# Graph attention at the two ends of a four-layer GNN: seven of sixteen row tiles computed row by row

## The chip, the cores and the metric

One core of a Trainium2 chip runs the whole program. The metric is device time in microseconds (us) from the first instruction to the last, the median of several executions. The engines named below are TensorE (PE), VectorE (DVE), ScalarE (ACT), GpSimd (POOL), and SyncE (SP), whose queue issues nearly all DMAs.

## What is computed

Eight graphs of 2048 nodes with 128 features share one 0/1 adjacency matrix. Four layers follow each other, each as `x = x + layer(relu(layernorm(x)))`. Layers 0 and 3 are graph attention with one head, layer 1 is masked attention with four heads, and layer 2 is a mean over neighbours. Layer 3, cut to what matters (layer 0 has the same score, and adds a second normalisation, a residual and an elu):

```python
h = einsum('bni,oi->bno', x, W)
s, d = h @ a_src, h @ a_dst
e = s[:, :, None] + d[:, None, :]
e = where(e > 0, e, 0.2 * e)
e = where(adj[None] == 0, -1e9, e)
out = einsum('bij,bjf->bif', softmax(e, axis=-1), h)
```

For each of the eight graphs that is a 2048 x 2048 score matrix, made from two vectors alone. A row tile is 128 rows of it, so there are 16 row tiles.

## The kernel before

**Order of the work.** Layer 1 of graph b is the backbone ("mains"). In its gaps the kernel lays layers 2 and 3 of graph b-1 and layer 0 of graph b+1. Two stretches have no such partner: layer 0 of graph 0 at the start, and layers 2 and 3 of graph 7 at the end. They are called the two ends here. The order of instructions on PE, DVE, ACT and POOL is the order in which the Python code emits them; each engine runs its list strictly in that order. The SP queue alone is ordered by the framework. It too waits at its first instruction that isn't ready.

**Graph attention, transposed (`gat_loop`).** Row tiles are taken in six groups of 3, 3, 3, 3, 2 and 2 (`GROUPS`). The score is held with the neighbour index j on the partitions and the group's rows along the free axis, so it can be used as a matmul operand without a transpose. One step handles two column tiles j (an item; there are 8 per group) and is skewed over seven stages:

- `leaky`: two ACT instructions (Prelu of row vector `ab` plus a bias per partition), 128x384 each for a group of three.
- `lowered`: DVE subtracts the row maximum, 128x768.
- `exps`: one ACT Exp, 128x768.
- `masked`: DVE applies the FP8 mask `mg`, 128x768.
- `product`: 6 PE matmuls into `gacc`; a column of ones in `haug` gives the softmax's sum.
- `ended` and `closed`: DVE divides and adds to x (`finish`), with an ACT Exp for layer 0's elu.

Five items can be in flight (pool `gp`, tile `ge`). Ahead of each group, `ahead` computes the row maxima (`gat_maximum`, line 447: one DVE instruction over 128x2048 for each row tile, from the row vector `s2b` and the int8 mask `pmg`, which a DMA fetches into two buffers of 256 KB), then `shifts` and `spread` send two short rows through DRAM and back as `ab` (line 410), on which the group's first `leaky` waits.

**Multi-head attention, by rows.** Layer 1 holds a score with its rows on the partitions: PE makes it, one masked minimum on DVE makes mask and maximum (line 963), one ACT Exp with the sum as a by-product (line 970), then PE transposes (line 982), ACT copies the transposed tiles out of PSUM as `eT` (line 987), and PE multiplies by the values.

**The start.** DMA brings 16 adjacency tiles of 1 MB. Each is turned into an int8 mask for rows (`pm_all`) and an FP8 mask for groups (`mg_all`) by DVE, PE and ACT (lines 1181 to 1211). The last of these steps are laid among the first steps of layer 0's loop. When a quarter of x (four row tiles) has ended, `before_attention` normalises and projects it for layer 1, in six short steps: statistics (DVE), root (POOL), apply (DVE), transpose, and two projections (PE, then ACT copies). Layer 1 can begin when all four quarters are projected.

**The end.** After layer 2 of graph 7, `layer3` projects, builds `s2b`, and the loop runs to the last output DMA.

Of the kernel before, what the change touches and what calls it, by code (L numbers as in the profile page):

```python
# [9 lines left out]
F32 = mybir.dt.float32  # L10
BF16 = mybir.dt.bfloat16
FP8 = mybir.dt.float8e4
I8 = mybir.dt.int8
# [18 lines left out]
def gnn_kernel(  # L32
# [104 lines left out]
    def chunk(s):  # L137

        return new(cp, "c", s, (P, 512))
# [90 lines left out]
    for c in range(2):  # L230
        nc.vector.tensor_scalar(
            ga[:, 2 * c : 2 * c + 2], a12_0, cols[:, 2 * T + 4 + c : 2 * T + 5 + c], None, ALU.mult
        )
    ones = const.tile([P, P], F32, name="ones")
    nc.gpsimd.memset(ones, 1.0)
    pga = psum("pga", (P, 4))
    nc.tensor.matmul(pga, ones, ga, start=True, stop=True)
    gab = const.tile([P, 4], F32, name="gab")
    nc.vector.tensor_copy(gab, pga)
    w0T = const.tile([P, P], F32, name="w0T")  # L240
    pw0 = psum("pw0", (P, P))
    nc.tensor.transpose(pw0, w0[:, 0:P], ident)
    nc.vector.tensor_copy(w0T, pw0)
# [33 lines left out]
    def at(place, f):  # L277

        f.place = place
        return f  # L280
# [19 lines left out]
    def run(steps):  # L300
        for _, fns in steps:
            settle()
            for f in fns:
                f()
        settle()
# [142 lines left out]
            dump, st["s2b"], pm, UP, HIGHEST, ALU.add, ALU.min, st["mn"][:, it : it + 1]  # L448
        )

    def gat_loop(st, finish, maxima, gap):


        steps = Steps()
# [34 lines left out]
            gr[k]["s1"], gr[k]["m"] = t[:, 0 : n * P], t[:, n * P : 2 * n * P]  # L489

        def ahead(k):
            if k >= len(GROUPS):
                return []
            return [
                [lambda: fetch(k), maximum_at(k, 0)],
                [lambda: fetch_mask(k, 0), maximum_at(k, 1)],
                [maximum_at(k, 2)],
                [lambda: shifts(k)],
                [lambda: spread(k)],
            ]  # L500
# [55 lines left out]
                for f in gr.pop(k)["close"]:  # L556
                    f()

        for fns in ahead(0):
            steps.add(2.0, *fns)  # L560

        items = []
        for k in range(len(GROUPS)):
            items += [(k, jp) for jp in range(T // 2)] + [None] * gap
        stages = [leaky, lowered, exps, masked, product, ended, closed]
        names = ["leaky", "lowered", "exps", "masked", "product", "ended", "closed"]
# [1 line left out]
        for step in range(len(items) + len(stages) - 1):  # L568
            fns = []
            if step < len(items) and items[step]:  # L570
                k, jp = items[step]
                if jp == 0:
                    nxt = ahead(k + 1)
                if 0 < jp <= len(nxt):
                    fns += nxt[jp - 1]
            for s in reversed(range(len(stages))):
                if 0 <= step - s < len(items) and items[step - s]:
                    fns.append(at(names[s], lambda f=stages[s], a=items[step - s]: f(*a)))
            steps.add(2.6, *fns)
        return steps  # L580

# [70 lines left out]
            steps.add(1.0, lambda it=it: gat_maximum(st, it))  # L652
        return steps

    def layer0_loop(b, st, maxima=False, gap=1):

        xb = xs[b]

        def finish(i0, n, acc, rec):
            hq = new(hpp, "hp", "hp", (P, 3, P))  # L660
            ex = new(hpp, "ex", "ex", (P, 3, P))
# [7 lines left out]
            def add():  # L669
                for q in range(n):  # L670
                    xg = xb[(i0 + q) // 4][:, (i0 + q) % 4, :]
                    nc.vector.scalar_tensor_tensor(xg, ex[:, q, :], 1.0, xg, ALU.min, ALU.add)
                    nc.vector.scalar_tensor_tensor(xg, hq[:, q, :], 0.0, xg, ALU.max, ALU.add)

            return [add]

        return gat_loop(st, finish, maxima, gap)

    attn, ready = {}, {}

# [168 lines left out]
        agg.add(1.0, lambda: combine(G - 1))  # L849
        return steps, agg  # L850

    def layer3(b, gap=1, maxima=True):
# [24 lines left out]

        pre = Steps()
        pre.skewed(
            G,  # L880
            norm_stages(lambda g: xb[g], hdst)
            + [turned, project],
            1.0,
        )
        pre.add(0.5, settle)
        pre.add(1.0, lambda: gat_ends(st), lambda: gat_rows(st))

        def finish(i0, n, acc, rec):
            for q in range(n):
                it = i0 + q  # L890
                xg = xb[it // 4][:, it % 4, :]
                nc.vector.scalar_tensor_tensor(
                    xg, acc[:, q, 0:P], rec[:, q : q + 1], xg, ALU.mult, ALU.add
                )
                if it % 4 == 3:
                    g = it // 4
# [6 lines left out]
        tops = [at("maxi", lambda it=it: gat_maximum(st, it)) for it in range(T)]  # L903
        return pre, gat_loop(st, finish, maxima, gap), tops

# [355 lines left out]
    with tc.manual_schedule(engines=ENGINES):  # L1261
# [13 lines left out]
        rest.add(1.0, late_constants)  # L1275
        run(rest)
        xb0 = xs[0]
        loop = layer0_loop(0, st0, True)
        quarters, queue, others = before_attention(0), [], masks_all[n:]
        start = len(loop) - 9 * len(GROUPS) - 6  # L1280
        for _ in range(3):
            run([others.pop(0)])
        n_late = len(others)
        for k, step in enumerate(loop):
            run([step])
            if others and (k + 1) * n_late >= 0.1 * len(loop) * (n_late - len(others)):
                run([others.pop(0)])
            for g, group in enumerate((1, 2, 3, 5)):
                if k == start + 9 * group + 13:
                    queue.extend(quarters([g]))  # L1290
            if queue:
                run([queue.pop(0)])
        run(others + queue)

        mains = []
# [74 lines left out]
        for b in range(B):  # L1370
            side = Steps()
            if b >= 1:
                pre2, agg = layer2(b - 1)
                side.extend(pre2)
                pre3, loop3, _ = layer3(b - 1, 0)
# [41 lines left out]
            work(side, (b + 1) * per + LAG if b + 1 < B else len(mains))  # L1417
        assert not pending
        pre2, agg = layer2(B - 1)
        pre3, loop3, _ = layer3(B - 1)  # L1420

        rest = Steps(pre2)
        ahead = list(pre3)
# [57 lines left out]
```

## Time and profile before

| | |
|---|---|
| median of 3 runs | 4548.66 us (4547.9 to 4550.93) |
| the profiled execution | 4556.48 us, its span 4554.6 us |
| mean granted TensorE clock | 0.956 of full speed |
| busy over the span | PE 88%, DVE 83%, ACT 79%, POOL 12% |
| start: first `leaky` to last `masked` | 109.4 to 239.5 us |
| last row tile of layer 0 done, first Exp of layer 1 | 243.3 us, 260.75 us |
| end: `s2b` in place, first `leaky` | 4423.8 us, 4438.6 us |
| end: last `masked`, output DMA issued, span ends | 4549.1, 4551.3, 4554.6 us |

The shares over the span are an average over unlike stages; in the middle PE is busy over 90% of most slices. The two ends, 5% of the span together, have to be read by themselves, with the busy time of each engine in slices of 20 us. A group in the list of instructions shows engine, line, operation, the tile written and read, the shape, how often, the busy sum and the mean of one, and the idle time just before it with what ended that. Instructions that follow each other on an engine overlap in the records by some 0.1 us, so that the distance from start to start is a little shorter than the mean.

### The profile page before, as it was taken

How to read it: one execution, taken by the hardware profiler on the slowest of the kernel's cores; microseconds unless marked ns; L12 is line 12 of the kernel's file. 1: busy time of each engine (PE TensorE's matmuls, PEld its weight loads, DVE VectorE, ACT ScalarE, POOL GpSimd, SP SyncE). 2: the span in 40 equal slices, each digit the busy share in tenths (PEclk: the TensorE clock that was granted, in tenths of full speed). 3: DMA queues.
4: the chain of work that ended last, by engine and by line, in shares of the span. 5: the costliest groups of instructions: out<-in, count | busy, mean ns of one | idle time of the engine just before them, and what ended most of it. 6: DMA issues, size and time to landing. Idle time of an engine off the chain costs nothing.

```text
span 4554.6 us, 87375 instructions
## 1 busy us (share of the span) xinstructions
PE 4009.2 (88%) x33290; PEld 2809.7 (62%) x33290; DVE 3796.6 (83%) x7529; ACT 3613.6 (79%) x5121; POOL 553.7 (12%) x549
## 2 busy tenths in 40 slices
PE   3679998998999989998899988999899989998966
PEld 2545765666657666576666756566665766655636
DVE  5968877889889898888988889799888898748939
ACT  6658985898859888698868988598895989858916
POOL 1220011004100130002300031001300010000000
PEclk6889999999999999999999999999999999999978
DMA  8522133223241323313242232412333223222232
GB/s 305 153 69 59 54 92 110 66 71 106 82 140 53 94 83 107 109 60 105 77 128 75 67 101 84 144 49 72 102 103 116 59 69 113 58 75 71 64 100 75
DMA packets 312192, 423.32 MB, mean 93 GB/s; under 512 B 65318, under 2 KB 181724, under 8 KB 307676
## 3 DMA queue, kind: packets, MB, share of 16 engines
q1 hardware_dynamic: 311264, 417.51, 30.2%
q8 instruction: 263, 4.31, 0.4%
q14 instruction: 157, 1.29, 0.1%
q10 hardware_dynamic: 508, 0.22, 0.0%
HBM read 365.78 MB, written 55.98 MB: 93 GB/s over the span
## 4 chain that ended last, share of the span: by engine, by line
PE 31%; DVE 25%; ACT 22%; issue 5%; DMA 2%; SPq 0%; DVEq 0%; POOL 0%; ACTq 0%
PE pagg L798 7%; DVE e L963 7%; ACT e L970 6%; PE pt L982 6%; ACT eT L987 6%; PE gacc L536 6%; DVE dump L447 5%; PE sc L946 5%; ACT ge L510 5%; DVE ge L516 4%; DVE ge L525 3%; PE acc L997 3%; ACT ge L520 3%; DVE ln_s L341 1%; PE ph L397 1%
## 5 line engine op out<-in xcount | busy, mean ns | idle before, releaser
L987 ACT COPY eT<-pt 128x1024 f32<-128x1024 f32 x1024 | 996.2, 1017 | 440.8 <-PE pt L982 439.5
L536 PE MATMUL gacc<-haug,ge 128*128 128x129 f32 x8192 | 1106.6, 285 | 156.4 <-DVE ge L525 121.5
L982 PE MATMUL pt<-ident,e 128*128 128x128 f32 x8192 | 1043.7, 279 | 168.6 <-DVE amh L963 126.1
L536 PEld LDWEIGHTS gacc<-haug,ge 128*128 128x128 f32 x8192 | 1008.2, 197 | 297.7 <-issue 215.3
L982 PEld LDWEIGHTS pt<-ident,e 128*128 128x128 f32 x8192 | 928.2, 144 | 268.5 <-DVE amh L963 149.8
L970 ACT ACTIVATE e<-e,amn 128x2048 f32<-128x2048 f32 x512 | 1035.1, 2022 | 12.7 <-DVE amn L963 12.7
L510 ACT ACTIVATE ge<-ab,s 128x384 f32<-128x384 f32 (+1 forms) x1536 | 808.0, 583 | 107.7 <-DMA ab<-rowd 89.2
L963 DVE CUSTOM_DVE_ANT_0 e<-sc,pm 128x1024 f32<-128x1024 f32 x512 | 625.0, 1221 | 265.6 <-PE sc L946 220.6
L946 PE MATMUL sc<-ks,qr 32*128 32x512 f32 x4096 | 746.6, 658 | 59.5 <-ACT eT L987 41.5
L963 DVE CUSTOM_DVE_ANT_0 e<-sc,pm,amh 128x1024 f32<-128x1024 f32 x512 | 657.5, 1284 | 76.0 <-PE sc L946 3.6
L520 ACT ACTIVATE ge<-ge 128x768 f32<-128x768 f32 (+1 forms) x768 | 601.3, 784 | 134.0 <-DVE ge L516 133.1
L525 DVE SCALAR_TENSOR_TENSOR ge<-mg,ge 128x768 f32<-128x768 fp8e4 (+1 forms) x768 | 666.3, 868 | 24.4 <-ACT ge L520 23.9
L516 DVE TENSOR_TENSOR ge<-ge,ab 128x768 f32<-128x768 f32 (+1 forms) x768 | 665.7, 867 | 16.3 <-ACT ge L510 13.1
L447 DVE CUSTOM_DVE_ANT_0 dump<-s2b,pmg 128x2048 bf16<-128x2048 f32 x256 | 588.9, 2300 | 36.9 <-DMA pmg<-pm_all 18.3
L997 PE MATMUL acc<-eT,vv 128*32 128x256 f32 x8192 | 562.9, 393 | 1.9 <-ACT eT L987 1.9
L997 PEld LDWEIGHTS acc<-eT,vv 128*32 128x32 f32 x8192 | 216.3, 110 | 496.4 <-issue 407.7
L349 POOL TENSOR_SCALAR ln_r<-ln_mv 128x4 f32<-128x4 f32 x128 | 86.4, 675 | 3528.2 <-DVE ln_mv L343 3280.7
L946 PEld LDWEIGHTS sc<-ks,qr 32*128 32x128 f32 x4096 | 235.3, 187 | 222.4 <-ACT eT L987 112.6
L798 PE MATMUL pagg<-mt,hm 128*128 128x512 fp8e4 x1536 | 353.6, 380 | 11.7 <-DVE agT L816 11.7
L798 PEld LDWEIGHTS <-hm 128*128 128x128 bf16 x1536 | 148.0, 98 | 185.5 <-issue 31.4
L350 POOL TENSOR_TENSOR ln_r<-ln_r,neg_half 128x4 f32<-128x4 f32 x128 | 161.4, 1261 | 10.7
L383 PE MATMUL ptr<-ident,h 128*128 128x128 f32 x512 | 88.2, 297 | 41.1 <-DVE h L357 12.6
(131 smaller groups left out, 2591.3 us busy)
## 6 DMA issues: line engine op xcount, KB each, us to landing
pmg<-pm_all SPq DMA_DIRECT2D x256, 256.0 KB
mg<-mg_all SPq DMA_DIRECT2D x128, 384.0 KB
pm<-pm_all SPq DMA_DIRECT2D x128, 256.0 KB
qr<-qd SPq DMA_DIRECT2D x1024, 32.0 KB
mt<-mt_all SPq DMA_DIRECT2D x64, 512.0 KB
ab<-rowd SPq DMA_DIRECT2D x64, 384.0 KB
adj<-in_adj_dram SPq DMA_DIRECT2D x16, 1024.0 KB
s2b<-rowd SPq DMA_DIRECT2D x16, 1024.0 KB
```

The source lines that it names most:

```text
L447: nc.vector.tensor_tensor_reduce(dump, st["s2b"], pm, UP, HIGHEST, ALU.add, ALU.min, st["mn"][:, it : it + 1])
L510: nc.scalar.activation(e[:, c, :], gr[k]["s1"], AF.Prelu, bias=st["s2"][:, j : j + 1], alpha=ALPHA)
L516: nc.vector.tensor_tensor(e, e, bc_mid(gr[k]["m"], 2), ALU.subtract)
L525: nc.vector.scalar_tensor_tensor(e, mt, BIG, e, ALU.mult, ALU.min)
L536: nc.tensor.matmul(gr[k]["acc"][:, q, :], e[:, c, q * P : (q + 1) * P], st["haug"][:, j, :], start=(j == 0 and q == 0), stop=(j == T - 1), ...
L798: nc.tensor.matmul(st["pa"], st["hm"][:, j, s, :], st["mt", g, j // 8][:, j % 8, :], start=(j == 0 and s == 0), stop=(j == T - 1 and s == ...
L946: nc.tensor.matmul(blk["sc"][g // 2][:, (g % 2) * 512 : (g % 2 + 1) * 512], blk["q"][r, t * P : (t + 1) * P], ks_t[b, hh][r, :], start=Tru ...
L963: nc.vector.tensor_tensor_reduce(e[:, c], blk["sc"][h], pm[:, c], UP, least, ALU.add, ALU.min, to)
L970: nc.scalar.activation(blk["e"][t], blk["e"][t], AF.Exp, scale=-1.0, bias=blk["mn"][:, t : t + 1], accum_out=blk["ao"]["sum"][:, t, blk["h ...
L982: nc.tensor.transpose(pt[:, c, t, :], blk["e"][t][:, j * P : (j + 1) * P], ident)
L987: nc.scalar.copy(eT, blk.pop(("pt", w)).rearrange("p c t n -> p c (t n)"))
L997: nc.tensor.matmul(pair["acc"][g * HD : (g + 1) * HD, blk["hh"] % 2, :], vv_t[blk["b"], blk["hh"]][:, j, :], blk["eT"][w][:, g, :], start= ...
```

## The change

At both ends the loop takes groups 0, 1 and 2 only (row tiles 0 to 8). Row tiles 9 to 15 go through a new function, `gat_rowwise`. `merged` lays its steps among those of `gat_loop`, spread over 90% of it at the start and 85% at the end. The empty slot between groups (`gap`) goes from 1 to 0 there. The six middle occurrences of each loop, and all else in the middle, keep their code and their order on PE, DVE, ACT and POOL.

For a row tile, `gat_rowwise` runs one Prelu over 128x2048 from `s2b` (ACT), one masked minimum over 128x2048 in place (DVE, the same instruction form as `gat_maximum`), one Exp over 128x2048 with the sum (ACT), 16 PE transposes, two PSUM copies of 128x1024 (ACT), 16 PE matmuls into `racc`, and a `finish` for one tile.

```diff
-    ones = const.tile([P, P], F32, name="ones")
+    ones = chunk("ones")[:, 0:P]
...
-    w0T = const.tile([P, P], F32, name="w0T")
+    w0T = chunk("w0T")[:, 0:P]
...
-    def gat_loop(st, finish, maxima, gap):
+    def gat_loop(st, finish, maxima, gap, ks=range(6)):
...
+    def gat_rowwise(st, finish, its):
+        e, eT, mn, acc, close, sm_ = {}, {}, {}, {}, {}, {}
+        def leaky(it):
+            if "s1n" not in st:
+                st["s1n"] = small("s1n", (P, T))
+                nc.vector.tensor_scalar(st["s1n"], st["s1"], -ALPHA / UP, None, ALU.mult)
+            e[it] = new(ep, "e", "er", (P, N))
+            nc.scalar.activation(
+                e[it], st["s2b"], AF.Prelu, scale=ALPHA, bias=st["s1n"][:, it : it + 1],
+                alpha=1.0 / ALPHA,
+            )
+        def lowest(it):
+            pm = new(mg, "pm", "pmg", (P, N), I8)
+            nc.sync.dma_start(out=pm, in_=pm_all[it])
+            mn[it] = small("rmn", (P, 1))
+            nc.vector.tensor_tensor_reduce(
+                e[it], e[it], pm, UP, HIGHEST, ALU.add, ALU.min, mn[it]
+            )
+        def exps(it):
+            sm_[it] = small("rsum", (P, 1))
+            nc.scalar.activation(
+                e[it], e[it], AF.Exp, scale=-1.0, bias=mn.pop(it), accum_out=sm_[it]
+            )
+        def turned(it, h):
+            pt = psum("ptg", (P, 8, P))
+            for c in range(8):
+                j = 8 * h + c
+                nc.tensor.transpose(pt[:, c, :], e[it][:, j * P : (j + 1) * P], ident)
+            def read():
+                eT[it, h] = new(tp, "eT", "eTg", (P, 8, P))
+                nc.scalar.copy(eT[it, h], pt)
+            later(read)
+        def product(it, h):
+            if h == 0:
+                acc[it] = new(psa, "acc", "racc", (P, 1, P))
+            t = eT.pop((it, h))
+            for c in range(8):
+                j = 8 * h + c
+                nc.tensor.matmul(
+                    acc[it][:, 0, :], t[:, c, :], st["haug"][:, j, 0:P],
+                    start=(j == 0), stop=(j == T - 1),
+                )
+        def ended(it):
+            rec = small("rrec", (P, 1))
+            nc.vector.reciprocal(rec, sm_.pop(it))
+            close[it] = finish(it, 1, acc.pop(it), rec)
...
+        stages = [
+            (7, closed), (6, ended), (0, leaky), (1, lowest), (2, exps),
+            (3, lambda i: turned(i, 0)), (4, lambda i: turned(i, 1)),
+            (4, lambda i: product(i, 0)), (5, lambda i: product(i, 1)),
+        ]
+        for step in range(2 * len(its) + 6):
...
-        return gat_loop(st, finish, maxima, gap)
+        return merged(
+            gat_loop(st, finish, maxima, gap, ks), gat_rowwise(st, finish, rest_of(ks)), share
+        )
...
-        loop = layer0_loop(0, st0, True)
+        loop = layer0_loop(0, st0, True, 0, [0, 1, 2], 0.9)
...
-            for g, group in enumerate((1, 2, 3, 5)):
-                if k == start + 9 * group + 13:
+            for g in range(G):
+                if g not in begun and st0["ended"].issuperset(range(4 * g, 4 * g + 4)):
+                    begun.add(g)
                     queue.extend(quarters([g]))
...
-        pre3, loop3, _ = layer3(B - 1)
+        pre3, loop3 = layer3(B - 1, 0, True, [0, 1, 2], 0.85)
```

A step number in `stages` counts steps of `gat_rowwise`; a new tile starts every second step. So an even step emits, for ACT, the Prelu of tile n and the Exp of tile n-1, and an odd step emits the masked minimum of tile n. A quarter of x now starts for layer 1 as soon as its four tiles have ended; quarters 1 and 2 need group 2 and so come last, one behind the other. Layer 3's output DMAs follow the same test.

More of the change, by code (lines that the diff above doesn't have):

```diff
@@ L491, in ahead @@
         def ahead(k):
-            if k >= len(GROUPS):
-                return []
             return [
@@ L557, in closed @@
                     f()
-        for fns in ahead(0):
+        for fns in ahead(ks[0]):
             steps.add(2.0, *fns)
         items = []
-        for k in range(len(GROUPS)):
+        for k in ks:
             items += [(k, jp) for jp in range(T // 2)] + [None] * gap
@@ L572, in gat_loop @@
                 if jp == 0:
-                    nxt = ahead(k + 1)
+                    nxt = ahead(ks[ks.index(k) + 1]) if k != ks[-1] else []
                 if 0 < jp <= len(nxt):
@@ L578, in gat_loop, with rest_of, closed @@
                     fns.append(at(names[s], lambda f=stages[s], a=items[step - s]: f(*a)))
+            steps.add(2.6, *fns)
+        return steps
+    def rest_of(ks):
+        its = set(range(T))
+        for k in ks:
+            its -= set(range(GROUPS[k][0], sum(GROUPS[k])))
+        return sorted(its)
+    def gat_rowwise(st, finish, its):
[44 more added lines that the diff above has]
+            close[it] = finish(it, 1, acc.pop(it), rec)
+        def closed(it):
+            for f in close.pop(it):
+                f()
+        stages = [
[3 more added lines that the diff above has]
+        ]
+        steps = Steps()
+        for step in range(2 * len(its) + 6):
+            fns = [
+                lambda f=f, i=its[(step - s) // 2]: f(i)
+                for s, f in stages
+                if (step - s) % 2 == 0 and 0 <= (step - s) // 2 < len(its)
+            ]
@@ L653, in layer0_maxima, with layer0_loop @@
         return steps
-    def layer0_loop(b, st, maxima=False, gap=1):
+    def layer0_loop(b, st, maxima=False, gap=1, ks=None, share=1.0):
         xb = xs[b]
         def finish(i0, n, acc, rec):
-            hq = new(hpp, "hp", "hp", (P, 3, P))
-            ex = new(hpp, "ex", "ex", (P, 3, P))
+            if n > 1:
+                hq = new(hpp, "hp", "hp", (P, 3, P))
+                ex = new(hpp, "ex", "ex", (P, 3, P))
+            else:
+                t = chunk("hp1")
+                hq, ex = (t[:, c * P : (c + 1) * P].unsqueeze(1) for c in range(2))
             for q in range(n):
@@ L669, in add @@
             def add():
+                ended.update(range(i0, i0 + n))
                 for q in range(n):
@@ L675, in finish @@
             return [add]
-        return gat_loop(st, finish, maxima, gap)
+        ended = st["ended"] = set()
+        if ks is None:
+            return gat_loop(st, finish, maxima, gap)
+        return merged(
+            gat_loop(st, finish, maxima, gap, ks), gat_rowwise(st, finish, rest_of(ks)), share
+        )
     attn, ready = {}, {}
@@ L850, in layer2, with layer3 @@
         return steps, agg
-    def layer3(b, gap=1, maxima=True):
+    def layer3(b, gap=1, maxima=True, ks=None, share=1.0):
         xb = xs[b]
@@ L894, in finish @@
                 )
-                if it % 4 == 3:
-                    g = it // 4
+                ended.add(it)
+                g = it // 4
+                if ended.issuperset(range(4 * g, 4 * g + 4)):
                     nc.sync.dma_start(
@@ L901, in finish @@
             return []
-        tops = [at("maxi", lambda it=it: gat_maximum(st, it)) for it in range(T)]
-        return pre, gat_loop(st, finish, maxima, gap), tops
+        ended = set()
+        if ks is None:
+            return pre, gat_loop(st, finish, maxima, gap)
+        loop = gat_loop(st, finish, maxima, gap, ks)
+        return pre, merged(loop, gat_rowwise(st, finish, rest_of(ks)), share)
     pending = []
@@ L1277, in gnn_kernel @@
         xb0 = xs[0]
-        loop = layer0_loop(0, st0, True)
+        loop = layer0_loop(0, st0, True, 0, [0, 1, 2], 0.9)
         quarters, queue, others = before_attention(0), [], masks_all[n:]
-        start = len(loop) - 9 * len(GROUPS) - 6
         for _ in range(3):
             run([others.pop(0)])
-        n_late = len(others)
+        n_late, begun = len(others), set()
         for k, step in enumerate(loop):
@@ L1292, in gnn_kernel @@
                 run([queue.pop(0)])
+        assert len(begun) == G
         run(others + queue)
@@ L1374, in gnn_kernel @@
                 side.extend(pre2)
-                pre3, loop3, _ = layer3(b - 1, 0)
+                pre3, loop3 = layer3(b - 1, 0)
             else:
```

## The prediction

> **What bounds the kernel now.** I looked first at the busy time of each engine in slices of 20 us, at both ends. Columns: stretch, length, then busy us (and count) of PE, PEld, DVE, ACT, POOL, then granted clock, DMA share and GB/s.
>
> ```profile
> 180.00:200.00 20.00, 12.81 (x90) 11.41 (x88) 19.86 (x42) 14.65 (x26) 5.73 (x4) 0.91 0.49 144
> ```
>
> That is the start; the end:
>
> ```profile
> 4440.00:4460.00 20.00, 12.30 (x84) 12.02 (x84) 20.00 (x26) 15.44 (x26) 0.00 (x0) 0.69 0.22 66
> 4460.00:4480.00 20.00, 12.44 (x87) 11.89 (x88) 19.96 (x29) 13.02 (x22) 0.00 (x0) 0.83 0.34 99
> 4480.00:4500.00 20.00, 12.02 (x80) 11.66 (x80) 19.96 (x29) 13.43 (x23) 0.00 (x0) 0.74 0.34 101
> ```
>
> DVE is full, ACT two thirds, PE under 65%. The waits of the end agree: ACT waits for DVE, and DVE hardly for anybody.
>
> ```profile
> ACT ge L520 <- DVE ge L516: 27.9, 20, 3.1
> ACT ge L510 <- DMA ab<-rowd: 23.4, 2, 23.1
> ...
> DVE ge L516 <- ACT ge L510: 6.2, 2, 5.7
> ```
>
> So a us taken from DVE there is a us of the end, until ACT is full. The prices are the groups of the end, one form each:
>
> ```profile
> L447 DVE CUSTOM_DVE_ANT_0 dump<-s2b,pmg 128x2048 bf16<-128x2048 f32 x16 | 36.6, 2286 | 8.2 <-DMA s2b<-rowd 7.6 <-DMA pmg<-pm_all 0.5
> L510 ACT ACTIVATE ge<-ab,s 128x384 f32<-128x384 f32 x64 | 35.1, 601 | 23.2 <-DMA ab<-rowd 23.1
> L516 DVE TENSOR_TENSOR ge<-ge,ab 128x768 f32<-128x768 f32 x32 | 30.5, 953 | 5.7 <-ACT ge L510 5.7
> L525 DVE SCALAR_TENSOR_TENSOR ge<-mg,ge 128x768 f32<-128x768 fp8e4 x32 | 30.3, 947 | 0.0
> L520 ACT ACTIVATE ge<-ge 128x768 f32<-128x768 f32 x32 | 26.9, 840 | 23.6 <-DVE ge L516 23.0
> L510 ACT ACTIVATE ge<-ab,s 128x256 f32<-128x256 f32 x32 | 14.1, 493 | 0.4 <-DMA ab<-rowd 0.4
> ```
>
> For the row-wise steps I take layer 1's ACT instructions from the list of the whole page:
>
> ```profile
> L987 ACT COPY eT<-pt 128x1024 f32<-128x1024 f32 x1024 | 996.2, 1017 | 440.8 <-PE pt L982 439.5
> ...
> L970 ACT ACTIVATE e<-e,amn 128x2048 f32<-128x2048 f32 x512 | 1035.1, 2022 | 12.7 <-DVE amn L963 12.7
> ```
>
> **Prices from start to start** (the timeline, where records overlap). An item of a three-tile group: DVE 0.87 + 0.87 = 1.74 us (4450.63 to 4452.37), ACT 2 x 0.53 + 0.75 = 1.81. A maximum 2.21 (4440.63 to 4442.84). A row-wise tile: its Exp with the sum 2.10 (4299.48 to the next start); two copies 1.80 (4297.69 to 4299.48). Two prices aren't shown. The Prelu over 2048: line 510 costs 493 ns at 256 and 601 at 384 elements, 0.84 ns each, so 2.0 at 2048, and the Exp row says 2.02; I take 1.93 start to start, bounds 1.9 to 2.1. The masked minimum in place: 2.21 by the row that reads SBUF, 2 x 1.28 = 2.57 by line 963, which reads PSUM; I take 2.21, the nearer row. A tile is then ACT 1.93 + 2.10 + 1.80 = 5.83, DVE 2.21 + 0.43 for dividing (layer 3). In a group of three a tile costs DVE 8 x 1.74 / 3 + 2.21 + 0.35 = 7.2.
>
> **PE** gets 16 transposes and 16 matmuls a tile where it had 16 matmuls: at 4296.56 sixteen transposes took 1.75 us at full clock, so 7 x 1.75 = 12 us more in 80 that had a third free. Half clock (0.50 after an idle stretch) doubles four transposes from 0.66 us (220.87) to 1.25 (246.24). The Trainium skill (TensorE: Matmul & The Clock Gate, Part 4: PE-mode transpose) speaks against the change here: transposes do not count as PE work and don't release the full clock. The trace grants 0.69 to 0.91 at the ends and 1.0 in layer 1, where transposes stand among the rest all the time. By the rule a tile's transposes would take twice the row's 1.75 us. The sum is the same by both, since Prelu and Exp, 4.0 us, stand on ACT between the transposes of one half and their copy.
>
> **The end, as a walk along the three queues.** I place each instruction of the new order after its predecessor on the engine and after what it reads. `s2b` lands at 4423.8 as before. DVE: two maxima, the minimum of tile 9 (its mask buffer refills at 4428.98, as the third maximum's did), the third maximum: the group's short rows leave at 4434.1 instead of 4431.9, and the DMA's 3.8 us behind them puts the first `leaky` at 4441.0 (was 4438.6). ACT has done two Prelus and an Exp by then. Left on ACT: 24 x 1.81 + 7 x 5.83 - 6.0 = 78.3 us. Left on DVE: 24 x 1.74 + 16 x 2.21 + 7 x 0.43 + 3 x 1.7 (dividing and shifts of a group) - 13.9 done ahead = 71.4. **ACT becomes the bound.** In the walk a cycle (a tile and some three items) takes ACT 11.35 us at first with no wait; after the turn of a group, where DVE has maxima and dividing too, ACT waits about 4 us in all. Last `masked` ends at 4441.0 + 78.3 + 4.1 + 0.9 = 4524.3. What follows took 5.5 us before (4549.1 to 4554.6); with a third tile in the last group 0.7 more: 4530.5. **The end gains 24.1 us.** With ACT fully covered it would be 28; at 10% waits 20.
>
> **The start.** First a loss. SP's new order puts the third maximum's mask behind the store of the last group mask (`mg_all`), which waits for ACT's last mask copy; that comes 2.1 us later (102.3) because a Prelu stands before it. So that maximum runs at 106 instead of 95.9, the block of node degrees with 16 small DVE operations (5.7 us, 98.8 to 104.5) now stands between it and the short rows, which leave at 114.2 instead of 98.9. Then the DMA of `ab` stands in SP behind a mask for the maximum of group 1 (free at 118.6), and needs 4.8 us: first `leaky` at 124, was 109.4. Behind it ACT has 84 us (as at the end, plus 7 x 0.3 and 2 x 0.5 for elu, plus 2.2 for one quarter), DVE 82. Here ACT also waits in each tile for the division just emitted on DVE (elu's Exp reads it in the same step), 0.3 to 2.6 us each in the walk; last `masked` ends at 217 instead of 239.5, 22.5 earlier. Then the tail is longer: before one quarter of x came behind the last group, now two, one behind the other: POOL adds a bias (1.26 us at 247, 7.6 at 175 beside a busy DVE) and takes a root (1.3) before the second apply (1.1); group 2 has six more short additions. Together 5 to 8; I take 7.5. **The start gains 15 us** (bounds 5 to 24).
>
> What hides costs: mask fetches for the row-wise tiles are as many as those maxima had (16), and group masks get fewer. `ones` and `w0T` moved pools: nothing, no instruction changes. `gap` 0: nothing where DVE was full across the turns.
>
> **Sum.** 15 + 24.1 = 39.1 us off the profiled 4556.5 (its span 4554.6 and 1.9 around it): 4517.4. That execution lies 7.8 above the median of the runs, so **4510 us** in those terms.
>
> **Rivals.**
> - *The hand-overs eat half.* ACT's queue now holds three kinds of work (loop, minimum, copies), each waiting for another engine; if every tile cycle loses 1.5 us more than in the walk, 14 cycles lose 21, or if the start's late `ab` isn't made up, 15 go. Gain 15 to 25: about **4529**. For: the loss at the start, a tight walk there. Against: one whole step of slack in `gat_loop`.
> - *The change doesn't shorten the ends*: the start is held by its DMAs (DMA share 0.95 at 80 to 100 us) and the end's new ACT bound costs as much as DVE did. Gain under 9: about **4545**. Against: 109 us of full DVE against 79 of ACT.
> - *Slower: ACT, in order, waits at the copies.* A copy of `eT` stands in front of the loop's `exps`; its transposes stand on PE behind products that wait for DVE, which waits for `exps`. One such circle per copy at half clock (8 transposes 1.75 + 8 matmuls 1.75 + the item's 1.81) is 5 us a tile, 14 x 5 = 70: 4510 + 70 = **4580**. It decides from 39.1 / 14 = 2.8 us a tile. Against: the walk finds the transposes done 2 us or more before their copy.
> - *Better*: ACT covered at both ends and a short tail, gain 52: **4496**, inside the forecast's margin.
>
> **How the numbers follow.** Forecast (4494 to 4523) 0.60, half eaten (4523 to 4538) 0.20, no shortening 0.08, slower 0.12. About 0.2%, 9 us, is what a measurement of this kernel can tell from no change. So faster 0.80, same 0.08, slower 0.12. The range takes the forecast and most of the first rival: 4490 to 4536.
>
> **What the profile after should show.** ACT over 90% busy and DVE under 90% between the first `leaky` and the last `exps` at the end; first `leaky` there some 17 us after `s2b`; at the start first `leaky` near 124, last `masked` near 217, first Exp of layer 1 near 246; layer 1's middle unchanged in length. Wrong if the Prelu or the in-place minimum costs over 2.6 us, if copies wait for transposes by the us, or if the start's first `leaky` comes after 130.

## The result, and the profile after

| | before | after |
|---|---|---|
| median of 4 runs | 4549.41 us (4547.90 to 4550.93) | 4515.54 us (4507.87 to 4520.93) |
| the profiled execution, its span | 4556.48, 4554.6 us | 4507.87, 4506.1 us |
| start: first `leaky`, last `masked` | 109.39, 239.50 us | 125.72, 218.00 us |
| first Exp of layer 1 | 260.75 us | 245.12 us |
| middle: from there to the end's first maximum | 4163.1 us | 4153.4 us |
| end: first maximum to first `leaky` | 14.8 us | 16.6 us |
| end: first `leaky` to last `masked`, and then to the span's end | 110.5, 5.5 us | 83.5, 7.5 us |

The change makes the kernel 0.8% faster: the ratio of the times is 0.9918, 95% interval 0.9905 to 0.9932, which is a gain of 31 to 43 us. The medians differ by 33.9 us; 39 were predicted. Two landmarks cut the span in three: the first Exp of layer 1, and the first masked maximum of the end (the instruction that has waited for `s2b`). The start is 15.6 us shorter, the end 23.2, together 38.8. The middle is 9.7 us shorter as well in these two executions, although nothing in it was changed.

Busy time by slices of 20 us at the end, after (PE, PEld, DVE, ACT, POOL, then granted clock, DMA share, GB/s):

```profile
4420.00:4440.00 20.00, 17.48 (x133) 16.93 (x132) 16.20 (x23) 20.00 (x29) 0.00 (x0) 0.84 0.29 81
4440.00:4460.00 20.00, 15.35 (x112) 14.99 (x111) 19.19 (x22) 17.51 (x22) 0.00 (x0) 0.84 0.28 85
4460.00:4480.00 20.00, 19.50 (x171) 19.06 (x171) 15.78 (x28) 18.36 (x25) 0.00 (x0) 0.99 0.13 40
4480.00:4500.00 20.00, 20.00 (x182) 20.00 (x181) 16.27 (x24) 15.81 (x25) 0.00 (x0) 1.00 0.09 27
```

DVE, which stood at 20.00 or 19.96 in every slice shown of before, has 16 to 19 now. ACT is full in the first slice, has a dip where the groups turn (4440 to 4460), and in the last slice has 15.81, less than DVE. And PE, a third free before, has no free time in that last slice. There it is PE that the others wait for:

```profile
4491.35 9.55 PE L534 MATMUL gacc<-haug,ge 128*128 128x129 f32 x84
...
4500.93 0.18 DVE L549 RECIPROCAL grec<-gacc 128x3 f32<-128x3 f32 x1 [2.31 <-PE gacc L534]
```

The start, in the slice that was shown of before:

```profile
180.00:200.00 20.00, 17.48 (x152) 16.87 (x152) 14.32 (x23) 19.04 (x28) 0.00 (x0) 1.00 0.22 67
```

ACT and DVE have changed places there: 19.04 and 14.32 instead of 14.65 and 19.86.

The waits of the end, after (engine, line and tile that waited, for whom: us, times, longest):

```profile
DVE ge L523 <- ACT ge L518: 8.9, 7, 2.4
...
ACT ge L508 <- DMA ab<-rowd: 7.1, 1, 7.1
...
ACT eTg L624 <- PE ptg L620: 4.6, 2, 4.1
```

The wait has turned round: ACT's `exps` waited 27.9 us for DVE before, now DVE's `masked` waits 8.9 us for ACT. The groups of the end, one form each, have the new prices:

```profile
L508 ACT ACTIVATE ge<-ab,s 128x384 f32<-128x384 f32 x48 | 26.9, 616 | 8.1 <-DMA ab<-rowd 7.1 <-PE gacc L534 1.0
...
L606 DVE CUSTOM_DVE_ANT_0 er<-er,pmg 128x2048 f32<-128x2048 f32 x7 | 16.0, 2284 | 0.9 <-DMA pmg<-pm_all 0.5 <-ACT er L597 0.4
...
L624 ACT COPY eTg<-ptg 128x1024 f32<-128x1024 f32 x14 | 14.1, 1007 | 4.6 <-PE ptg L620 4.6
L612 ACT ACTIVATE er<-er,rmn 128x2048 f32<-128x2048 f32 x7 | 14.0, 2003 | 1.1 <-DVE rmn L606 1.1
L597 ACT ACTIVATE er<-s2b,s1n 128x2048 f32<-128x2048 f32 x7 | 13.9, 1999 | 10.6 <-DVE s1n L594 10.6
```

The masked minimum in place costs 2284 ns in the records, as much as the maximum of line 447 (2287), and the Prelu over 2048 costs 2.00 us.

### The profile page after: what moved, and what is told of

It reads as the page before. It is cut to its first block, busy times and chain, and to the rows that moved or that the text cites. A ratio compares the mean times of both kernels' runs of the same rounds, so it can differ in the third digit from the quotient of the medians.

```text
span 4506.1 us, 87571 instructions
## 1 busy us (share of the span) xinstructions
PE 4010.4 (89%) x33514; PEld 2818.9 (63%) x33514; DVE 3728.0 (83%) x7419; ACT 3618.1 (80%) x5051; POOL 532.8 (12%) x549
## 4 chain that ended last, share of the span: by engine, by line
PE 32%; DVE 23%; ACT 23%; issue 5%; DMA 1%; SPq 0%; DVEq 0%; POOL 0%; ACTq 0%
PE pagg L890 7%; DVE e L1059 7%; ACT e L1066 7%; PE pt L1078 7%; PE gacc L534 6%; ACT eT L1083 6%; ACT ge L508 5%; PE sc L1042 5%; DVE dump L447 5%; DVE ge L514 3%; PE acc L1093 3%; ACT ge L518 3%; DVE ge L523 3%; DVE ln_s L341 1%; PE ph L397 1%
## 5 line engine op out<-in xcount | busy, mean ns | idle before, releaser
L534 PE MATMUL gacc<-haug,ge 128*128 128x129 f32 x7744 | 1026.2, 282 | 41.8 <-DVE x L984 17.3
L1066 ACT ACTIVATE e<-e,amn 128x2048 f32<-128x2048 f32 x512 | 1035.6, 2023 | 14.2 <-DVE amn L1059 14.2
L534 PEld LDWEIGHTS gacc<-haug,ge 128*128 128x128 f32 x7744 | 934.7, 194 | 172.3 <-issue 114.9
L508 ACT ACTIVATE ge<-ab,s 128x384 f32<-128x384 f32 (+1 forms) x1440 | 763.5, 588 | 95.3 <-DMA ab<-rowd 78.0
L523 DVE SCALAR_TENSOR_TENSOR ge<-mg,ge 128x768 f32<-128x768 fp8e4 (+1 forms) x720 | 628.6, 873 | 36.4 <-ACT ge L518 36.2
L518 ACT ACTIVATE ge<-ge 128x768 f32<-128x768 f32 (+1 forms) x720 | 568.8, 792 | 88.9 <-DVE ge L514 88.6
L514 DVE TENSOR_TENSOR ge<-ge,ab 128x768 f32<-128x768 f32 (+1 forms) x720 | 625.5, 869 | 16.0 <-ACT ge L508 12.3
L447 DVE CUSTOM_DVE_ANT_0 dump<-s2b,pmg 128x2048 bf16<-128x2048 f32 x242 | 556.9, 2301 | 44.1 <-DMA pmg<-pm_all 24.5
```

Of the source, the lines that this page charges most:

```text
L447: nc.vector.tensor_tensor_reduce(dump, st["s2b"], pm, UP, HIGHEST, ALU.add, ALU.min, st["mn"][:, it : it + 1])
L508: nc.scalar.activation(e[:, c, :], gr[k]["s1"], AF.Prelu, bias=st["s2"][:, j : j + 1], alpha=ALPHA)
L514: nc.vector.tensor_tensor(e, e, bc_mid(gr[k]["m"], 2), ALU.subtract)
L523: nc.vector.scalar_tensor_tensor(e, mt, BIG, e, ALU.mult, ALU.min)
L534: nc.tensor.matmul(gr[k]["acc"][:, q, :], e[:, c, q * P : (q + 1) * P], st["haug"][:, j, :], start=(j == 0 and q == 0), stop=(j == T - 1), ...
L1066: nc.scalar.activation(blk["e"][t], blk["e"][t], AF.Exp, scale=-1.0, bias=blk["mn"][:, t : t + 1], accum_out=blk["ao"]["sum"][:, t, blk["h ...
```

## The experiments

All kernels by the same landmarks, each from one profiled execution. "Start" is the first Exp of layer 1, "end" runs from the first maximum to the span's end. Each ratio is to runs of the kernel before that were measured beside it; their medians lie between 4549.2 and 4553.9 us, so the medians in the table can't be compared with 4549.4 alone.

| kernel | first `leaky` | start | middle | end | median | ratio to before, 95% |
|---|---|---|---|---|---|---|
| before | 109.4 | 260.8 | 4163.1 | 130.8 | 4549.4 | |
| after | 125.7 | 245.1 | 4153.4 | 107.6 | 4515.5 | 0.9905 to 0.9932 |
| e1_end_only | 109.8 | 260.2 | 4160.7 | 107.8 | 4527.6 | 0.9928 to 0.9957 |
| e2_start_only | 126.0 | 245.9 | 4163.6 | 130.3 | 4537.6 | 0.9954 to 0.9980 |
| e4_act_more | 125.6 | 249.3 | 4159.6 | 111.6 | 4522.6 | 0.9918 to 0.9951 |
| e5_dve_more | 126.8 | 274.8 | 4155.8 | 124.3 | 4564.7 | 1.0019 to 1.0038 |
| e5b_dve_plain | 126.7 | 249.5 | 4160.3 | 108.7 | 4521.1 | 0.9926 to 0.9956 |
| e8_pe_more | 125.4 | 244.4 | 4160.4 | 108.4 | 4513.9 | 0.9909 to 0.9940 |
| e3_short_rows_first | 109.2 | 242.0 | 4170.2 | 107.2 | 4518.6 | 0.9911 to 0.9944 |
| e3b_degrees_late | 118.9 | 244.4 | 4166.3 | 107.5 | 4520.0 | 0.9918 to 0.9947 |
| e9_degrees_in_gap | 107.5 | 237.3 | 4163.8 | 108.2 | 4512.6 | 0.9895 to 0.9925 |
| e6_split6_10 | 126.7 | 242.8 | 4155.3 | 104.9 | 4505.1 | 0.9877 to 0.9910 |
| e7_split12_4 | 122.4 | 258.5 | 4160.1 | 116.9 | 4541.1 | 0.9960 to 0.9982 |
| e10_joined | 109.7 | 247.7 | 4166.2 | 105.5 | 4521.0 | 0.9912 to 0.9939 |

Where a kernel leaves an end as it is, the length of that end repeats within a us: the five kernels with the end of the changed kernel (itself among them) show 107.2 to 108.2. The middle differs by up to 17 us. So the ends are read from the landmarks, and differences of a few us in the medians are not read at all.

The theory to be tested was: the two ends are separate; at each, ACT is the bound now, DVE has some 7 us of slack, and PE has slack but for the last 10 us.

### Each end by itself

```diff
-        loop = layer0_loop(0, st0, True, 0, [0, 1, 2], 0.9)
+        loop = layer0_loop(0, st0, True)
```

> The start keeps the loop of before with all six groups; the end is changed. Theory (the gain is the sum of two separate ends, about 15.6 us at the start and 23.2 at the end, and the 10 us by which the middle of the profiled execution was shorter is drift): about 23 us less than before, 4526, the end from the landing of s2b to the span's end 107 to 108 us, and the start as before, first Exp of layer 1 near 261. Rival (the changed start also shortens the middle, since layer 1 is begun with other quarters ready): the middle goes back by 10 us to 4163, and the gain of the end alone is the same 23, so that the start is worth 25. Rival (the change doesn't shorten the end, the time came from elsewhere): within 5 us of before.

```diff
-        pre3, loop3 = layer3(B - 1, 0, True, [0, 1, 2], 0.85)
+        pre3, loop3 = layer3(B - 1)
```

> The end keeps the loop of before; the start is changed. Theory (two separate ends): about 15 us less than before, 4534; first Exp of layer 1 near 245, the end from the landing of s2b to the span's end near 131, and the middle between them as long as before within the drift of single executions. Rival (the start shortens the middle too): 25 us less, 4524, the middle near 4153. Rival (start without effect): within 5 us of before.

Measured beside the same runs of before (4551.8): the end alone gains 24.3 us, the start alone 14.2, together 38.5. Each end has its landmark of the changed kernel and leaves the other as it was. The middles are 4160.7 and 4163.6 us, so neither change brings the 4153.4 of the changed kernel's profile. That the changed start shortens the middle isn't borne out. The 9.7 us lie within the spread of single executions: the four runs of the changed kernel lie 13 us apart.

### A price for each engine

One more ACT copy, one more DVE instruction, or eight more transposes for each of the seven row-wise tiles.

```diff
                 nc.scalar.copy(eT[it, h], pt)
+                if h == 1:
+                    nc.scalar.copy(eT[it, h], pt)
```

> Each row-wise tile copies its second half out of PSUM twice, on ACT: 14 more copies of about 0.9 us, 6.3 us of ACT at each end, the result unchanged. Theory (ACT is the bound of both ends now): about 6 us more at each end than the changed kernel, so the end from s2b to the span's end near 113, the first Exp of layer 1 near 251, 4528 in all. Rival (PE is the late one, since it was busy without a break in the last 20 us): under 2 us at each end, 4517. Rival (DVE still bounds): also under 2, and then the same work on DVE shows it.

The start is 4.2 us longer, the end 4.0, for 6.3 us of ACT: two thirds of the price (about 6 at each end were expected). ACT is the engine that counts, but not all of the time: at the end its wait for transposes fell from 4.6 to 1.8 us.

```diff
                 nc.scalar.copy(eT[it, h], pt)
+                if h == 1:
+                    spare = new(op, "dump", "dump", (P, N), BF16)
+                    nc.vector.tensor_copy(
+                        spare[:, 0:1024].rearrange("p (c n) -> p c n", c=8), pt)
```

> The same second copy of half 1, but on DVE into a spare tile: 14 copies of about 1.1 us, 7.7 us of DVE at each end, the result unchanged. Theory (ACT bounds, DVE has 7 us of slack at each end: 71.4 against 78.3): 0 to 3 us more at each end than the changed kernel, 4516 to 4521. Rival (both engines full by turns, so that any work on either one costs its whole price): 6 to 8 us at each end, 4530. Rival (PE is the bound): under 1.5 us at each end.

All three theories missed it. The start is 29.7 us longer, the end 16.7, for 8.6 us of DVE work each. The group of the copies in the end:

```profile
L627 DVE CAST dump<-ptg 128x1024 bf16<-128x1024 f32 x7 | 8.6, 1225 | 19.8 <-ACT eTg L624 19.8
```

and one of them in the timeline (start, us, what, and the idle time before it):

```profile
4508.07 1.04 PE L620 MATMUL ptg<-ident,er 128*128 128x128 f32 x8
...
4508.93 0.35 DVE L987 SCALAR_TENSOR_TENSOR x<-racc,rrec,x 128x128 f32<-128x128 f32 x1
...
4512.58 0.99 ACT L624 COPY eTg<-ptg 128x1024 f32<-128x1024 f32 x1
...
4513.60 1.23 DVE L627 CAST dump<-ptg 128x1024 bf16<-128x1024 f32 x1 [4.33 <-ACT eTg L624]
```

The transposes that DVE's copy reads have ended at 4509.1, but the copy starts at 4513.60, 0.03 us after ACT's copy of the same tile; ACT's copy stands behind a Prelu and an Exp in its own queue. Six of the seven at the end wait like that, all seven at the start. So it is not the work that costs (8.6 us), it is that DVE's in-order queue now waits nearly once a tile for the other queue: 19.8 us at the end, 29.7 at the start, and ACT then waits for DVE in turn (14.7 us at `exps` in the end). This run could not tell how much slack DVE has, so the copy was replaced by work on data that has long been there:

```diff
-                    nc.vector.tensor_copy(
-                        spare[:, 0:1024].rearrange("p (c n) -> p c n", c=8), pt)
+                    s2b = st["s2b"]
+                    nc.vector.tensor_tensor(
+                        spare[:, 0:1024], s2b[:, 0:1024], s2b[:, 1024:2048], ALU.subtract)
```

> In the place of the second copy that cost 51 us, DVE gets a subtraction of two halves of s2b into the same spare tile: 7 more of about 1.23 us at each end, 8.6 us of DVE each, from data that has been in SBUF for long, so that it waits for nothing. Theory (the 51 us of that run were waits, 29.7 and 19.8 us at the copy itself, and DVE has slack at both ends): 1 to 4 us more at each end than the changed kernel; s2b to the span's end 108.5 to 112, first Exp of layer 1 near 247 to 249, all in all 4517 to 4523. Rival (DVE itself is the bound beside ACT and any DVE work costs its price): 8 us at each end, s2b to the span's end near 116. Rival (each DVE instruction in this place delays a hand-over and costs more than its price): over 10 at each end.

Seven subtractions of 1.216 us: the end is 1.1 us longer, the start 4.4. So the same time of DVE without the wait costs little, and DVE has slack at the end, as the theory has it. At the start half of its work counts: 4.4 us, just over the 1 to 4 of the theory.

```diff
+            for c in range(8 * h):
+                j = 8 * h + c
+                nc.tensor.transpose(pt[:, c, :], e[it][:, j * P : (j + 1) * P], ident)
```

> Each row-wise tile does the eight transposes of its second half twice, into the same PSUM tile: 56 more PE instructions at each end, 7 times 1.04 to 1.8 us, 8 to 12 us of PE, the result unchanged; ACT and DVE get nothing more. Theory (PE has slack but for the last 10 us): 0 to 3 us more at each end than the changed kernel, s2b to the span's end 108 to 111, 4516 to 4521. Rival (PE, busy without a break in the last 20 us, is the real bound of the end's second half): 5 to 10 us at the end, and less at the start. Rival (the copies of eT on ACT are late by what their transposes take longer): about 1 us for each tile, 7 at each end, with waits of ACT at ptg.

The 56 transposes take 8.1 us of PE at the end, which is 0.8 us longer; the start is 0.7 shorter, so nothing. Over either end as a whole PE is not the bound, however full its slices look. Three slices of the end of this run, as far from its first maximum as the last three of the changed kernel:

```profile
4446.30:4466.30 20.00, 17.92 (x162) 17.71 (x161) 18.62 (x22) 18.77 (x24) 0.00 (x0) 1.00 0.29 85
4466.30:4486.30 20.00, 18.60 (x168) 18.44 (x167) 16.07 (x28) 18.05 (x25) 0.00 (x0) 1.00 0.12 40
4486.30:4506.30 20.00, 20.00 (x182) 20.00 (x182) 16.53 (x24) 15.46 (x25) 0.00 (x0) 1.00 0.09 27
```

With half as many transposes again the granted clock is 1.00 in all three; the changed kernel had 0.84, 0.99 and 1.00 in the same three. PE's busy time at the end grew by 3.1 us, less than the added work, and the other matmuls took less time (`racc` 30.7 us instead of 32.4). That holds for the slices before the last. In the last one PE was full at a clock of 1.00 in both kernels, and there the run doesn't show that PE has room: ACT's last copy waited 1.7 us for its transposes instead of 0.5, and DVE's last reciprocal waited 2.3 us for the products in both.

### The start's late first `leaky`

```diff
-        return merged(
-            gat_loop(st, finish, maxima, gap, ks), gat_rowwise(st, finish, rest_of(ks)), share
-        )
+        loop = gat_loop(st, finish, maxima, gap, ks)
+        out = Steps(loop[:5])
+        out.extend(merged(Steps(loop[5:]), gat_rowwise(st, finish, rest_of(ks)), share))
+        return out
...
-            if others and (k + 1) * n_late >= 0.1 * len(loop) * (n_late - len(others)):
+            late = len(others) > 1 or k > len(loop) // 2
+            if others and late and (k + 1) * n_late >= 0.1 * len(loop) * (n_late - len(others)):
```

> At the start the five steps that run ahead of group 0 (masks, maxima, shifts, short rows) come before any row-wise step, and the block of node degrees is put off to the second half of the loop; the end is that of the changed kernel. Theory (the first leaky comes 16 us later than before because the third maximum's mask and the degrees stand ahead of the short rows): ab is issued near 104 again, first leaky near 110, 15 us earlier; ACT has then done two Prelus and an Exp less ahead of it (6 us), so the start ends 6 to 9 us earlier, first Exp of layer 1 near 237, 4507 in all. Rival (the start is held by its DMAs, whose share is 1.0 at 80 to 100 us, and whatever comes earlier waits there): first Exp of layer 1 stays within 2 us of 245. Rival (the degrees, put off, are then in the way of the loop): over 245.

The second of these two edits alone (`late`, with the loop merged as in the changed kernel):

```diff
+            late = len(others) > 1 or k > len(loop) // 2
+            if others and late and (k + 1) * n_late >= 0.1 * len(loop) * (n_late - len(others)):
```

> Only the block of node degrees is put off to the second half of the start's loop; the row-wise steps still stand among those that run ahead of group 0. Theory: the 5.7 us of the block go from in front of the short rows, which leave at 108.5 instead of 114.2; first leaky near 120, first Exp of layer 1 near 240 to 242, 4511 in all. Rival (the third maximum's mask, behind the store of the last group mask in SP, is what counts, or the DMAs are full): first leaky within 2 us of 125.7 and no gain.

In the changed kernel the cause of the late `ab` is in DVE's timeline:

```profile
95.28 2.28 DVE L606 CUSTOM_DVE_ANT_0 er<-er,pmg 128x2048 f32<-128x2048 f32 x1
...
105.87 2.29 DVE L447 CUSTOM_DVE_ANT_0 dump<-s2b,pmg 128x2048 bf16<-128x2048 f32 x1 [8.30 <-DMA pmg<-pm_all]
...
109.59 4.27 DVE L1330 SCALAR_TENSOR_TENSOR hbs<-bneigh,has,bself 128x128 f32<-128x128 f32 x16
...
114.16 0.21 DVE L404 STREAM_TRANSPOSE row<-cab 128x32 f32<-128x32 f32 x1
```

8.3 us for the third maximum's mask, then 5.7 for the degrees, then the short rows. With the degrees out of the way the first `leaky` comes 6.9 us earlier, with both out of the way 16.5. But the start gains only 0.8 and 3.1 us, and its first Exp stands at 244.4 and 242.0, where 240 to 242 and 237 were expected. Of the 16.5, some 6 were expected to go, since two Prelus and an Exp no longer run ahead of the loop. ACT's timeline of the run with short rows first shows what else stands against it:

```profile
160.72 1.11 ACT L508 ACTIVATE ge<-ab,s 128x384 f32<-128x384 f32 x2
170.27 0.31 ACT L753 ACTIVATE hp<-hp 128x128 f32<-128x128 f32 x1 [8.44 <-DVE hp L749]
```

The block of degrees now stands on DVE at 164.1 to 169.7, in the middle of the loop, and ACT's next instruction is elu's Exp, which reads a division behind that block: a hole of 8.4 us. Most of what was gained ahead of the loop was given back in it, as the rival on the degrees has it, though its number (over 245) isn't reached. DVE stood idle from 99.2 to 110.3 in that run, waiting for the first Prelu; so the block was put there:

```diff
-            late = len(others) > 1 or k > len(loop) // 2
+            late = len(others) > 1 or k >= 4
```

> The run with short rows first, with one thing moved: the block of node degrees comes right behind the short rows of group 0, where DVE stood idle for 11 us waiting for the first Prelu. Theory (bringing first leaky 16.5 us forward gave only 3.1 because the block, put in the loop, held DVE for 5.7 us there and ACT for 8.4): ACT's hole of 8.4 us goes, first leaky stays near 110, first Exp of layer 1 at 234 to 237, 8 to 11 us earlier than the changed kernel, 4506 to 4509 in all. Rival (what is bound at the start is the mask traffic or the tail, and the hole only moves): first Exp of layer 1 at 240 to 242, as in that run. Rival (the block's stores stand in SP before the fetch of ab): first leaky 3 us or more later.

```profile
96.91 0.21 DVE L404 STREAM_TRANSPOSE row<-cab 128x32 f32<-128x32 f32 x1
97.05 0.13 DVE L1316 TENSOR_SCALAR cnt<-nsum 128x16 f32<-128x16 f32 x1
...
98.52 4.26 DVE L1331 SCALAR_TENSOR_TENSOR hbs<-bneigh,has,bself 128x128 f32<-128x128 f32 x16
...
108.66 0.96 DVE L514 TENSOR_TENSOR ge<-ge,ab 128x768 f32<-128x768 f32 x1 [3.59 <-ACT ge L508]
```

The degrees are done before `ab` lands, the first `leaky` is at 107.5, and the start ends at 237.3: 7.8 us earlier than in the changed kernel, 4.7 earlier than with the degrees in the loop. The foretold 234 to 237 is missed by 0.3. Moving the block alone is thus worth 4.7 us, not the 8.4 of the hole. The median (4512.6) shows less of it than the landmark does; its middle was 4163.8. Whether the middle of the four kernels that move the degrees (this one, the two above, and the last of the study: 4163.8 to 4170.2; the others 4153.4 to 4163.6) is longer for a reason, such as work of layer 1 that waits for something else, stays open.

### Other shares for the two ways

Ten tiles by rows at both ends, or four (`[0, 1, 2, 3]` in the same two places):

```diff
-        loop = layer0_loop(0, st0, True, 0, [0, 1, 2], 0.9)
+        loop = layer0_loop(0, st0, True, 0, [0, 1], 0.9)
...
-        pre3, loop3 = layer3(B - 1, 0, True, [0, 1, 2], 0.85)
+        pre3, loop3 = layer3(B - 1, 0, True, [0, 1], 0.85)
```

> Both ends with groups 0 and 1 in the loop and ten row tiles by rows instead of seven. By the prices three tiles change DVE by -13.7 us and ACT by +3.0 at each end. Theory (ACT bounds, a us of it costs two thirds, as the second copy showed): 2 to 3 us more at the end than the changed kernel, s2b to the span's end 109 to 111, and the same at the start. Rival (the waits between the engines count as much as ACT's sum, and a loop with less DVE loses them, also one change of groups less): 2 to 4 us less at the end, near 104.

> Both ends with groups 0 to 3 in the loop and four row tiles by rows. By the prices DVE gets 13.7 us more at each end (85 against ACT's 75). Theory (DVE becomes the bound again): the end 7 to 9 us longer than the changed kernel's, s2b to the span's end 115 to 117, the start 4 to 9 later, 4528 in all. Rival (DVE's slack is as wide as the plain subtraction showed, 8.6 us for 1.1): the end near 110, 4518.

Four tiles by rows make DVE the bound again:

```profile
4460.00:4480.00 20.00, 13.66 (x86) 12.80 (x86) 19.88 (x30) 15.11 (x23) 0.00 (x0) 0.74 0.23 73
4480.00:4500.00 20.00, 17.14 (x137) 16.74 (x136) 19.93 (x27) 16.26 (x26) 0.00 (x0) 0.91 0.27 86
```

The end is 9.3 us longer than the changed kernel's (7 to 9 were expected), the start 13.4 (4 to 9). Ten tiles by rows are better, not worse: the end 2.7 us shorter, the start 2.3. Here the theory's sum fails, and the rival's number (near 104; it is 104.9) holds, by a wait that it did not name. ACT before and around the first `leaky` of the end, with ten tiles:

```profile
4410.54 2.00 ACT L597 ACTIVATE er<-s2b,s1n 128x2048 f32<-128x2048 f32 x1
4412.44 1.99 ACT L612 ACTIVATE er<-er,rmn 128x2048 f32<-128x2048 f32 x1
...
4414.43 1.00 ACT L624 COPY eTg<-ptg 128x1024 f32<-128x1024 f32 x1
4416.88 1.12 ACT L508 ACTIVATE ge<-ab,s 128x384 f32<-128x384 f32 x2 [1.46 <-DMA ab<-rowd]
```

and with seven:

```profile
4407.85 0.19 ACT L612 ACTIVATION_READ_ACCUMULATOR er<-er,rmn 128x1 f32 x1
4415.14 1.12 ACT L508 ACTIVATE ge<-ab,s 128x384 f32<-128x384 f32 x2 [7.11 <-DMA ab<-rowd]
```

With more row-wise steps in the same share of a shorter loop, a second tile is under way before `ab` lands. ACT waits 1.5 us there instead of 7.1, which pays for the 3 us that three tiles add and leaves 2.6. The whole end agrees: ACT is busy for 85.60 us instead of 82.53 and idle for 19.3 instead of 25.1. At the start it is of the same kind: ACT waits 6.9 us for `ab` instead of 21.5, with another Prelu, another Exp and two copies done ahead.

### Joined

Ten tiles by rows at both ends, short rows first, degrees behind them:

```diff
-        loop = layer0_loop(0, st0, True, 0, [0, 1, 2], 0.9)
+        loop = layer0_loop(0, st0, True, 0, [0, 1], 0.9)
...
+        out = Steps(loop[:5])
+        out.extend(merged(Steps(loop[5:]), gat_rowwise(st, finish, rest_of(ks)), share))
...
+            late = len(others) > 1 or k >= 4
...
-        pre3, loop3 = layer3(B - 1, 0, True, [0, 1, 2], 0.85)
+        pre3, loop3 = layer3(B - 1, 0, True, [0, 1], 0.85)
```

> The two edits that helped, joined: at the start short rows first with the degrees behind them, and ten row tiles by rows in place of seven at both ends. Theory (the two gains are of different kinds, waits ahead of the loop there and ACT's wait for ab filled here): at the start first leaky near 108 and first Exp of layer 1 at 234 to 237, at the end 104.9 us from s2b to the span's end as with ten tiles, about 4500 in all, 10 to 16 us under the changed kernel. Rival (with the short rows early there is no wait at the start left to fill, and three more tiles cost ACT 3 us): first Exp of layer 1 at 238 to 241, 4503. Rival (the row-wise tiles hold up the quarters of x, which then stand behind one another in the tail): over 241.

The third rival holds. The first `leaky` is at 109.7, but the start ends at 247.7, 2.5 us later than in the changed kernel and 4.9 later than with ten tiles alone. Three quarters of x normalise one behind the other on DVE:

```profile
221.32 1.11 DVE L357 TENSOR_SCALAR h<-x,ln_mv,ln_r 128x128 f32<-128x128 f32 x4
...
225.13 1.11 DVE L357 TENSOR_SCALAR h<-x,ln_mv,ln_r 128x128 f32<-128x128 f32 x4 [1.63 <-POOL ln_r L350]
...
228.94 1.12 DVE L357 TENSOR_SCALAR h<-x,ln_mv,ln_r 128x128 f32<-128x128 f32 x4 [1.64 <-POOL ln_r L350]
```

The row-wise steps begin only behind the five first steps here, so their last tile is divided at 215.4, and the quarter that it completes joins the two that wait for group 1. With ten tiles alone the three applies are at 215.8, 222.0 and 225.8. And from the end of the last one to the first Exp of layer 1 it is 17.6 us here, 15.9 with ten tiles alone, 14.0 in the changed kernel; why the stretch behind the last apply differs wasn't traced. The end has its 105.5. The start of `e9_degrees_in_gap` with the end of `e6_split6_10` is the version that these landmarks point to; it was not run. Of those that were run, ten tiles by rows is the fastest: 4505.1 us, though its interval (0.9877 to 0.9910) touches that of the changed kernel.

## Why the prediction was right, step by step

- **The end** was to gain 24.1 us and gained 23.2. First `leaky` 17 us after `s2b`: 16.6. From there to the last `masked` 78.3 + 4.1 + 0.9 = 83.3: it is 83.5, but as 76.5 of ACT's work + 5.9 of its waits (4.6 for the copies, 1.3 for others) + 1.0. That a work term 1.8 us too long and a wait term 1.8 us too short cancel is luck. ACT over 90% and DVE under 90% in between: from 4415.1 to 4496.5 ACT has 75.69 of 81.36 us (93%), DVE 69.08 (85%).
- **The tail of the end** was to be 6.2 us and is 7.5. The step "7 x 1.75 = 12 us more in 80 that had a third free" gave PE too much room at the very end: the products of the last group run in one stretch up to 4500.9, and the reciprocal waits 2.3 us for them (1.4 before).
- **The start** was to gain 15 and gained 15.6: first `leaky` 124 (125.7), last `masked` 217 (218.0), first Exp of layer 1 246 (245.1). The loss ahead of the loop has the sizes that were foretold, the maximum at 106 (105.9), the degrees 5.7, the short rows at 114.2 (114.16). One step towards them didn't happen: ACT's last mask copy was to end 2.1 us later, at 102.3, because of the Prelu, and ended at 100.3 (100.2 before). The third maximum's mask did go out behind the store of that copy, but 5.6 us passed from the copy's end to the maximum where 3.7 had been allowed, so that 106 came out right by luck. The tail is 5.9 us longer than before, not 7.5, which makes up for the first `leaky` that came 1.7 late.
- **The prices**: the in-place minimum is the SBUF row's (2284 ns), not the PSUM row's 2.57; the Prelu is 2.00 us in the records and 1.89 from start to start (4418.08 to 4419.97; 1.93 was taken). The Exp with the sum is 2.00 from start to start, not 2.10: in the trace of before the next instruction of ACT stands at 4301.48. An item costs ACT 1.74 (4489.30 to 4491.04; 1.81 was taken). These differences are enough for a work term that was 1.8 us too long.
- **The clock.** Before, the slices of the ends lay between 0.50 (4420 to 4440) and 1.00 (220 to 240), wider than the 0.69 to 0.91 that were read. After, row first: where transposes alternate with products the clock was 1.00 (from 4462 to 4482), and eight transposes took 1.04 us; at the end 0.50 was seen behind idle stretches of PE and for 6 to 9 us of work after them: at 4408, where sixteen took 3.68 us behind 18.4 us of idle PE, then from 4416 to 4426, and from 4454 to 4460 behind 3.6 us. The Trainium skill (TensorE: Matmul & The Clock Gate, Part 4: PE-mode transpose) has transposes not count as PE work in the same way. Among matmuls these runs show no such cost: 56 more of them left the clock at 0.90 or above in the end's last four slices. Transposes by themselves for longer than 3.68 us don't occur at this end, so what they would do alone isn't shown.
- **The slower rival** (ACT waits at a copy whose transposes stand behind a product that waits for DVE) happened once at the end, for 4.1 us (the copy at 4461.6; the products ahead of its transposes had waited 3.6 us for DVE and ran at a clock of 0.50), not 5 us a tile (the sum 14 x 5 counted one circle a tile, though a tile has two copies). The other wait at a copy is 0.5 us. A circle of a similar kind can cost that much: with a copy on DVE that stood behind ACT's, the two ends lost 46.4 us, more than the 38.8 that the whole change had gained.
- **The total** of 4510 lies 5.5 us under the median. The two ends gain 38.8 us in the profiles, where 39.1 had been forecast, and 38.5 in the runs with one end each. The 5.5 us can't be told from noise: the interval of the gain is 31 to 43 us, and the changed kernel's own runs spread over 13.
- **What was wrong in the reasoning**, though not in the number: "a us taken from DVE there is a us of the end, until ACT is full" and "ACT becomes the bound". A us of ACT costs two thirds, at the start a us of DVE still costs half, and in the last 10 us of the end PE is the one that is waited for. ACT's sum counts only behind the first `leaky`; ten tiles by rows raise the sum and still win, because work moves into a wait that seven tiles left empty.

## What to carry to other kernels

When one of two coupled in-order engines is full and the other isn't, a second algorithm for part of the same work could be priced here by the sum of each queue from the trace, with the first wait of each queue placed by hand; some of the closeness was luck. After the change the sum was not the whole bound any more. What helped was to look for the stretch in which both engines wait for a transfer, and to put work there that the loop would otherwise carry (a block of small operations moved out of the loop into that stretch gained 4.7 us). An instruction that waits for another engine at nearly each step of a full queue cost a multiple of its work, here 16.7 and 29.7 us for 8.6.

## What the runs showed that had not been expected

- 8.1 us of added transposes made the end only 0.8 us longer. PE had free time before the last slice, and there the granted clock was higher with them (0.90 to 1.00 instead of 0.84 to 1.00) and the other matmuls took less time. Why the clock was higher isn't shown; PE also stood idle in other places. In the last slice, where PE has 20.00 of 20.00 us in both kernels, the clock was 1.00 in both and PE had no room.
- The length of the unchanged middle varies from 4153 to 4170 us between kernels, while the unchanged ends repeat within 1 us. Whole times of single kernels hide a gain of 5 us that the landmarks show.
